# The first steps of a two-stream graph network in another written order

## The chip, the cores and the metric

The kernel runs on one core of one Trainium2 chip. The metric is the device time of one execution in microseconds; lower is better. Several runs of the same kernel are taken and their median is compared.

## The reference

There are 16 graphs (B) of 1024 nodes (N) with 128 features (C), and 4 layers (L) in each of two networks. All inputs are float32, and the adjacency holds zeros and ones.

```
h = relu(layernorm(x))
for i in range(4):                       # gated network
    m = adj^T @ (h @ weight[i])
    h = gru(m, h, w_ih[i], w_hh[i], b_ih[i], b_hh[i])
x = x + h * mask
h = relu(layernorm(x))
for i in range(4):                       # convolution with batch norm
    h = relu(adj @ (h @ W[i]) + b[i])
    h = gamma[i] * (h - mean) / sqrt(var + eps) + beta[i]   # over all graphs and nodes
x = x + h
```

In the GRU cell r and z are sigmoids, n is a tanh, and the new state is (1 - z) n + z h.

## The kernel before, in words

Features lie turned (channels on the 128 partitions, nodes along the free axis) for the gates, and by node for the aggregation. A 1024 x 1024 adjacency is held as 8 row tiles of 128 x 1024. The features are split into a high part in a reduced float format and a low part, both multiplied with the rows (`aggregate`, L511 to L522; 32 matmuls of 512 columns), so that the sum keeps float32 accuracy. That is exact only if the adjacency's values fit the reduced format; a "look" (L566 to L570, a maximum over the low 16 bits of a row on VectorE) records this for each of the 128 row tiles, and a general path that is not taken here stands behind it.

The gated network runs two streams, A (`sa`, even graphs) and B (`sb`, odd graphs), half a layer apart: while one stream aggregates, the other computes its gates. `gate_step` (from L700) makes six products for half of the nodes in four accumulators `g_r`, `g_hn`, `g_xn`, `g_z`; ScalarE takes the sigmoids (L730, L734) and the tanh (L733), VectorE the rest (L731, L732, L736 to L738). `half_step` repeats for the 16 graphs and 4 layers. The convolution follows, layer by layer over all graphs.

The change touches the opening alone, which is written out by hand for streams A and B with graphs 0 and 1. In it every engine works its queue in the order written (a manual schedule for all five engines); behind the opening only GpSimd and the DMA queue of SyncE are fixed, and a planner orders the other three. What the opening has to do:

- Load the x of both graphs, the small vectors (biases, scales, the mask: `load_small`, L431, issued on ScalarE's queue), the rows of graph 0, and the weights of layer 0. The first four rows of a graph land in a buffer `stage`, the other four in buffers of the tag `h`. The rows of graph 1 go to `stage` as well, one by one as those of graph 0 have been looked at and copied.
- Copy the rows to the reduced format (`open_rows`): those of graph 0 on GpSimd (0 to 3) and ScalarE (4 to 7), all of graph 1 on GpSimd.
- Norm both x (`norm_stats` on VectorE, then root, reciprocal, scale, and eight relus on ScalarE, four to a half), and split each half of y (`split_first`: a copy on ScalarE, L697, and a difference on VectorE, L698).
- Turn the small vectors on TensorE and copy them out on VectorE (`turn_small`: `vecs`, `brz`, `maskT`, L445 to L452), turn y of both graphs (`turn`, L603), and turn and combine the gate weights (`turn_layer`, L463 to L481: three copies to VectorE, one product, a fourth copy). All turns share two PSUM buffers.
- Fetch the x of graph 2 on GpSimd's queue, behind the row copies of graph 1 (`sa.ahead`; its issue is L531), for the norm that the planner puts beside the first gates.

At the very start TensorE turns the identity 52 times while it has nothing to do.

Of the kernel before, what the change touches and what calls it, by code (L numbers as in the profile page):

```python
# [16 lines left out]
P = 128  # L17
# [324 lines left out]
def exact_path(  # L342
# [21 lines left out]
    nc = tc.nc  # L364
    B, N, C = x.shape
    L = g_weight.shape[0]
    NB = N // P
    NH = N // HALF
    BH = HALF // P
# [12 lines left out]
    def tmp(name):  # L382
        return ps_t.tile([P, HALF], F32, tag="tmp", name=name)
# [5 lines left out]
    def flat(name):  # L389
        return keep.tile([P, NB, C], F32, tag="x", name=name, bufs=4)  # L390
# [10 lines left out]
    def hw_tiles(b, name):  # L401
        return [keep.tile([P, N], F32R, tag=f"hw{b % 2}{s}", name=f"{name}_{s}") for s in range(2)]


    ident = const.tile([P, P], F32, tag="ident", name="ident")
# [25 lines left out]
    def load_small(prep):  # L431

        vn = prep.tile([P, C], F32, tag="vn", name="vn", bufs=1)[:NV, :]
        r0 = 0
        for src in (g_b_ih, g_b_hh):
            nc.scalar.dma_start(vn[r0 : r0 + 3 * L, :], src.rearrange("l (g c) -> (l g) c", c=C))
            r0 += 3 * L
        for src in (c_b, c_gamma, c_beta):
            nc.scalar.dma_start(vn[r0 : r0 + L, :], src)
            r0 += L  # L440
        mn = prep.tile([P, P], F32, tag="mn", name="mn", bufs=1)
        nc.scalar.dma_start(mn, nodemask.rearrange("b (k p) -> (b k) p", p=P))
        return vn, mn

    def turn_small(vn, mn):  # L445
        pt = tmp("pt_v")
        nc.tensor.transpose(pt[:, :NV], vn, ident[:NV, :NV])
        nc.vector.tensor_copy(vecs, pt[:, :NV])
        nc.vector.tensor_add(brz, vecs[:, : 3 * L], vecs[:, 3 * L : 6 * L])
        pt = tmp("pt_m")  # L450
        nc.tensor.transpose(pt[:, :P], mn, ident)
        nc.vector.tensor_copy(maskT, pt[:, : B * NB])  # L452
# [72 lines left out]
    with ExitStack() as st:  # L525
# [3 lines left out]
        def load_x(b, eng):  # L529
            xt = flat(f"x{b}")  # L530
            eng.dma_start(xt, x[b].rearrange("(k p) c -> p k c", p=P))  # L531
            return xt
# [3 lines left out]
        def gru_row(b, j):  # L536
            if j < 6:
                return row_tile(f"row{b}_{j}")
            return work.tile([P, N], F32R, tag="row2", name=f"row{b}_{j}", bufs=4)

        def load_rows_first(b, stage):

            fs = []
            for j in range(NB):
                if j < 4:
                    f = stage[:, 2 * j : 2 * j + 2, :].rearrange("p a n -> p (a n)")
                else:
                    f = work.tile([P, N], F32, tag="h", name=f"first{b}_{j}", bufs=7)
                nc.sync.dma_start(f, adj[b][j * P : (j + 1) * P, :])
                fs.append(f)  # L550
            return fs
# [14 lines left out]
        def look(b, row, j):  # L566

            lows = row.bitcast(U16).rearrange("p (n t) -> p n t", t=2)[:, :, 0]
            k = b * NB + j
            nc.vector.tensor_reduce(low[:, k : k + 1], lows, axis=AX.X, op=ALU.max)  # L570
# [11 lines left out]
        def norm_stats(xt, name):  # L582
            stats = small.tile([P, NB, 6], F32, tag="ln_st", name=f"st_{name}")
            mv = small.tile([P, NB, 2], F32, tag="ln_mv", name=f"mv_{name}")
            for k in range(NB):
                nc.vector.bn_stats(stats[:, k, :], xt[:, k, :])
                nc.vector.bn_aggr(mv[:, k, :], stats[:, k, :])
            return mv

        def norm_apply(xt, y, name, mv, split=None):  # L590
            rs = small.tile([P, NB], F32, tag="ln_rs", name=f"rs_{name}")
            nc.scalar.activation(rs, mv[:, :, 1], AF.Sqrt, bias=eps_t)
            nc.vector.reciprocal(rs, rs)
            ms = small.tile([P, NB], F32, tag="ln_ms", name=f"ms_{name}")
            nc.vector.scalar_tensor_tensor(ms, mv[:, :, 0], -1.0, rs, ALU.mult, ALU.mult)
            for k in range(NB):
                nc.scalar.activation(
                    y[:, k * P : (k + 1) * P], xt[:, k, :], AF.Relu, bias=ms[:, k : k + 1], scale=rs[:, k : k + 1]
                )
                if split and k % BH == BH - 1:  # L600
                    split(k // BH)

        def turn(y, name, hT=None):  # L603

            if hT is None:
                hT = work.tile([P, N], F32, tag="h", name=f"h_{name}", bufs=7)
            for hf in range(NH):
                pt = tmp(f"pt_{name}_{hf}")
                for q in range(BH):
                    k = hf * BH + q  # L610
                    nc.tensor.transpose(pt[:, q * P : (q + 1) * P], y[:, k * P : (k + 1) * P], ident)
                nc.scalar.copy(hT[:, hf * HALF : (hf + 1) * HALF], pt)
            return hT
# [31 lines left out]
        class Stream:  # L645
# [5 lines left out]
            def open(self, xt):  # L651

                self.xt = xt
                self.y = work.tile([P, N], F32, tag=f"y{self.tag}", name=f"y_in{self.b}", bufs=1)
                self.mv = norm_stats(xt, f"in{self.b}")

            def open_split(self):

                self.hw = hw_tiles(self.b, f"ghw{self.b}_0")
                norm_apply(self.xt, self.y, f"in{self.b}", self.mv, self.split_first)  # L660

            def open_rows(self, fs, on_scalar):
                self.rows, self.looks = [], NB
                for j, f in enumerate(fs):
                    t = gru_row(self.b, j)
                    if j in on_scalar:
                        nc.scalar.copy(t, f)
                    else:
                        nc.gpsimd.tensor_copy(t, f)
                    self.rows.append(t)  # L670

            def prepare(self, b, xt):
# [126 lines left out]
        sa, sb = Stream(0), Stream(1)  # L799
        every = {getattr(mybir.EngineType, e) for e in ("PE", "DVE", "Activation", "Pool", "SP")}  # L800
        with tc.tile_pool(name="prep", bufs=1) as prep, tc.manual_schedule(engines=every):


            pt = tmp("pt_idle")
            for k in range(52):
                nc.tensor.transpose(pt[:, k % 4 * P : (k % 4 + 1) * P], ident, ident)
            x0, x1 = load_x(0, nc.sync), load_x(1, nc.sync)
            small_in = load_small(prep)
            stage = keep.tile([P, NB, N], BF16, tag="adjT", name="stage", bufs=1).bitcast(F32)
            rows0 = load_rows_first(0, stage)  # L810
            h0 = work.tile([P, N], F32, tag="h", name="h_in0", bufs=7)
            load_layer(0)
            w_g = flat("w_g")[:, :L, :]
            nc.sync.dma_start(w_g, g_weight.rearrange("l c d -> c l d"))

            sa.open(x0)
            sa.open_split()
            sb.open(x1)
            sa.open_rows(rows0, (4, 5, 6, 7))
            sa.agg_step(0)  # L820
            for j, f in enumerate(rows0):
                look(0, f, j)
            rows1 = load_rows_first(1, stage)
            for i in range(1, L):
                load_layer(i)
            h1 = work.tile([P, N], F32, tag="h", name="h_in1", bufs=7)
            sa.agg_step(1)
            turn_small(*small_in)
            turn(sa.y, "in0", h0)
            turn_layer(prep, w_g, 0)  # L830
            sa.hT = h0
            sb.open_split()
            turn(sb.y, "in1", h1)
            sb.hT = h1
            sb.open_rows(rows1, ())
            nc.gpsimd.dma_start(w_c, c_w.rearrange("l c d -> c l d"))
            sa.gate_step(0)
            sa.gate_step(1)
            sb.agg_step(0)
            sb.agg_step(1)  # L840
            for j, f in enumerate(rows1):
                look(1, f, j)
            for i in range(1, L):
                turn_layer(prep, w_g, i)
            sa.ahead()
        with tc.manual_schedule(engines={mybir.EngineType.Pool, mybir.EngineType.SP}):
            for s in range(1, B // 2 * L):
                half_step(sa, sb)
                half_step(sb, sa)
            sb.gate_step(0)  # L850
            sb.gate_step(1)
            with tc.issue_after(sb.last_act.ins):
                sa.rest()
            sb.finish()
# [4 lines left out]
    pt = tmp("pt_flag")  # L859
# [134 lines left out]
    for b in range(B):  # L994
        hT = conv_input(b, L, aff)
        for hf in range(NH):
            tag = turns[(b * NH + hf) % len(turns)]
            pt = tmp(f"pt_o{b}_{hf}") if tag == "tmp" else acc(tag, f"pt_o{b}_{hf}")
            for q in range(BH):
                k = hf * BH + q  # L1000
# [56 lines left out]
```

## Time and profile before

| | us |
|---|---|
| median of 3 runs | 1886.74 (1886.47 to 1887.95) |
| the profiled execution | 1884.96 |
| its span, first to last instruction | 1883.2 |
| TensorE busy with matmuls | 1826.3 (97%) |
| VectorE busy | 1209.0 (64%) |
| ScalarE busy | 1041.8 (55%) |
| GpSimd busy | 287.5 (15%) |
| mean granted TensorE clock | 0.986 |

The profile is of one execution. It names engines PE (TensorE matmul), PEld (its weight loads), DVE (VectorE), ACT (ScalarE), POOL (GpSimd) and SP (SyncE, which only issues DMAs); a q behind the name means the queue of DMA issues. Times count from the first instruction. A wait is named after what ended it. A busy TensorE is not TensorE at its peak, since the ends of matmuls are modelled. The opening with the gates of graph 0 takes the first 50 us of the span.

### The profile page before, as it was taken

The page shows a single profiled execution, that of the slowest core. Times are in us where ns is not written, and L with a number is a line of the kernel's source. Part 1 is how long each engine was busy: PE and PEld are TensorE (multiplying, and loading weights), DVE is VectorE, ACT ScalarE, POOL GpSimd, SP SyncE. Part 2 cuts the span into 40 slices and gives each one's busy share as a digit, 9 for nine tenths or more (in the row PEclk, how much of TensorE's full clock was granted, in tenths as well). Part 3 has the DMA queues.
Part 4 walks back from the last instruction along what each step waited for, and adds up shares of the span by engine and source line. Part 5 has one row for each costly group of instructions (what it writes and reads, how often), then busy time and mean ns, then how long its engine had stood idle before and what let it go on. Part 6 is the DMA issues. An engine that isn't in the chain of part 4 may idle for free.

```text
span 1883.2 us, 21902 instructions
## 1 busy us (share of the span) xinstructions
PE 1826.3 (97%) x7324; PEld 1259.9 (67%) x7324; DVE 1209.0 (64%) x2235; ACT 1041.8 (55%) x1561; POOL 287.5 (15%) x369
## 2 busy tenths in 40 slices
PE   7999999999999999999999999999989989989995
PEld 4666656666656566656665666667768878878884
DVE  5746864865784685595586476576656656665664
ACT  4354563563545454445456353476767767767764
POOL 3130230231141032033023012010100000000021
PEclk8999999999999999999999999999999999999997
DMA  7487476385386476557547536269956757675768
GB/s 258 120 229 255 157 203 216 140 223 170 134 256 189 147 190 202 200 168 234 190 157 203 208 114 169 85 220 319 305 187 214 246 179 246 223 247 180 250 208 259
DMA packets 267824, 381.21 MB, mean 202 GB/s; under 512 B 149716, under 2 KB 171896, under 8 KB 263864
## 3 DMA queue, kind: packets, MB, share of 16 engines
q1 hardware_dynamic: 250032, 246.21, 43.2%
q0 software_dynamic: 17456, 133.45, 20.2%
q8 instruction: 59, 0.97, 0.2%
q14 instruction: 61, 0.50, 0.1%
q10 hardware_dynamic: 216, 0.08, 0.0%
HBM read 287.39 MB, written 117.44 MB: 215 GB/s over the span
## 4 chain that ended last, share of the span: by engine, by line
PE 44%; issue 5%; DMA 3%; DVE 2%; POOL 1%; ACT 1%; SPq 0%; DVEq 0%; POOLq 0%; ACTq 0%
PE pc_m L516 12%; PE pc_g_r L516 5%; PE pc_g_z L516 5%; PE pm L516 5%; PE hw_c L493 5%; PE g_z L720 2%; PE g_r L720 2%; DMA adjT<-half 2%; PE g_xn L720 1%; PE g_hn L720 1%; PE pt_o L1001 1%; PE pw_g_hn L931 1%; PE pw_g_xn L931 1%; PE pc_g_r L503 1%; PE hw_g L491 0%
## 5 line engine op out<-in xcount | busy, mean ns | idle before, releaser
L516 PE MATMUL pm<-row,ghw 128*128 128x512 f32 x2048 | 505.0, 403 | 1.7 <-ACT ghw L697 1.7
L516 PEld LDWEIGHTS pm<-row,ghw 128*128 128x128 f32 x2048 | 383.4, 188 | 107.0 <-issue 31.6
L516 PE MATMUL pc_m<-wide,chw 128*128 128x512 f32 x1024 | 247.6, 396 | 0.0
L516 PEld LDWEIGHTS pc_m<-wide,chw 128*128 128x128 f32 x1024 | 190.7, 189 | 41.5 <-issue 3.8
L733 ACT ACTIVATE r<-r,vecs 128x512 f32<-128x512 f32 x128 | 92.3, 721 | 203.5 <-DVE r L732 203.4
L516 PE MATMUL pc_g_r<-wide,chw 128*128 128x512 f32 x464 | 185.8, 400 | 0.0
L516 PE MATMUL pc_g_z<-wide,chw 128*128 128x512 f32 x464 | 180.8, 390 | 0.0
L575 POOL CAST half<-row 128x1024 bf16<-128x1024 f32 x128 | 139.9, 1109 | 248.8 <-DMA adjT<-half 167.8
L878 DVE CAST wide<-packed 128x1024 fp32r<-128x1024 bf16 x160 | 110.5, 694 | 81.9 <-PE pc_m L516 62.4
L878 DVE CAST wide<-block 128x1024 fp32r<-128x1024 bf16 x160 | 110.4, 693 | 80.0 <-PE pc_g_z L516 42.2
L734 ACT ACTIVATE z<-g_z,brz 128x512 f32<-128x512 f32 x128 | 87.4, 683 | 121.5 <-PE g_z L720 121.5
L496 DVE TENSOR_TENSOR ghw<-hw_g,ghw 128x512 fp32r<-128x512 f32 x96 | 61.7, 683 | 122.7 <-ACT ghw L495 122.7
L720 PE MATMUL g_xn<-m,w_mT 128*128 128x512 f32 x256 | 131.7, 596 | 3.9 <-DVE r L732 3.9
L876 ACT CAST wide<-packed 128x1024 fp32r<-128x1024 bf16 x96 | 100.6, 1048 | 60.7 <-PE pc_g_z L516 30.1
L876 ACT CAST wide<-block 128x1024 fp32r<-128x1024 bf16 x96 | 100.6, 1048 | 60.2 <-PE pc_m L516 34.0
L720 PE MATMUL g_r<-m,w_mT 128*128 128x512 f32 x256 | 131.2, 594 | 0.0
L570 DVE TENSOR_REDUCE low<-row 128x1 f32<-128x1024 uint16 x112 | 130.9, 1201 | 0.0
L720 PE MATMUL g_z<-m,w_mT 128*128 128x512 f32 x256 | 130.7, 592 | 0.0
L730 ACT ACTIVATE r<-g_r,brz 128x512 f32<-128x512 f32 x128 | 87.8, 686 | 61.1 <-PE g_r L720 60.0
L736 DVE TENSOR_TENSOR h<-h,r 128x512 f32<-128x512 f32 x96 | 69.6, 725 | 78.7 <-ACT r L733 78.7
L731 DVE SCALAR_TENSOR_TENSOR r<-g_hn,vecs,r 128x512 f32<-128x512 f32 x128 | 95.1, 743 | 36.4 <-PE g_hn L720 19.1
L708 ACT COPY m<-pm 128x512 f32<-128x512 f32 x128 | 68.1, 583 | 89.4 <-PE pm L516 89.4
(128 smaller groups left out, 2767.8 us busy)
## 6 DMA issues: line engine op xcount, KB each, us to landing
packed<-adjT_d SPq DMA_DIRECT2D x256, 256.0 KB, 5.7
block<-adjT_d SPq DMA_DIRECT2D x256, 256.0 KB, 5.3
raw<-in_adj_dram POOLq DMA_DIRECT2D x112, 512.0 KB, 11.6
row<-raw SPq DMA_DIRECT2D x112, 512.0 KB, 6.1
adjT_d<-adjT POOLq DMA_DIRECT2D x16, 2048.0 KB, 7.2
xmid_d<-x POOLq DMA_DIRECT2D x16, 512.0 KB, 4.1
y<-ymid_d POOLq DMA_DIRECT2D x16, 512.0 KB, 6.1
xo<-xmid_d POOLq DMA_DIRECT2D x32, 256.0 KB, 6.4
```

The costliest lines, as they stand in the source:

```text
L493: nc.tensor.matmul(pt[:, q * P : (q + 1) * P], src, w, start=True, stop=True)
L516: nc.tensor.matmul(pm[hf], hw[s][:, j * P : (j + 1) * P], rows[j][:, hf * HALF : (hf + 1) * HALF], start=(j == 0 and s == 0), stop=(j == N ...
L570: nc.vector.tensor_reduce(low[:, k : k + 1], lows, axis=AX.X, op=ALU.max)
L575: nc.gpsimd.tensor_copy(t, row.bitcast(F32))
L720: nc.tensor.matmul(po, wT[:, i, g * C : (g + 1) * C], rhs, start=start, stop=stop)
L730: nc.scalar.activation(r, pr, AF.Sigmoid, bias=brz[:, 3 * i : 3 * i + 1])
L731: nc.vector.scalar_tensor_tensor(r, phn, b_hn(i), r, ALU.add, ALU.mult)
L733: nc.scalar.activation(r, r, AF.Tanh, bias=b_in(i))
L734: self.last_act = nc.scalar.activation(z, pz, AF.Sigmoid, bias=brz[:, 3 * i + 1 : 3 * i + 2])
L736: nc.vector.tensor_sub(ho, hin, r)
L876: nc.scalar.copy(r, t)
L878: nc.vector.tensor_copy(r, t)
```

## The change

- The turns of the small vectors move to the front: ahead of the first norm on TensorE and VectorE. Of the 52 idle turns 20 stand ahead of them and 28 behind.
- The looks at the rows of graph 0 no longer stand together behind the second graph's statistics: rows 0 and 1 are looked at between the first norm's scale and its first half, row 2 between the halves, rows 3 to 7 behind the second graph's scale.
- The second graph's scale and the first half of its norm stand ahead of the first aggregation's evacuation, its split and second half behind the turn of the first graph's y.
- The turn of the second graph's y moves behind the first gates.
- The looks at the rows of graph 1 leave the manual schedule: the planner places them, not before the last gate operation of graph 0.

`norm_apply` is cut into `norm_scale` and `norm_half` for this, and `open_split` becomes `open_half`; `open_rows` takes the row numbers and the engine of the copies, which stay as they were. No arithmetic changes.

```diff
-        def norm_apply(xt, y, name, mv, split=None):
+        def norm_scale(name, mv):
             rs = small.tile([P, NB], F32, tag="ln_rs", name=f"rs_{name}")
...
             nc.vector.scalar_tensor_tensor(ms, mv[:, :, 0], -1.0, rs, ALU.mult, ALU.mult)
-            for k in range(NB):
+            return rs, ms
+
+        def norm_half(xt, y, scale, hf):
+            rs, ms = scale
+            for k in range(hf * BH, (hf + 1) * BH):
                 nc.scalar.activation(
                     y[:, k * P : (k + 1) * P], xt[:, k, :], AF.Relu, bias=ms[:, k : k + 1], scale=rs[:, k : k + 1]
                 )
-                if split and k % BH == BH - 1:
-                    split(k // BH)
...
+            def open_half(self, g):
+
+                norm_half(self.xt, self.y, self.scale, g)
+                self.split_first(g)
...
-            for k in range(52):
-                nc.tensor.transpose(pt[:, k % 4 * P : (k % 4 + 1) * P], ident, ident)
+            def idle(n):
+                for k in range(n):
+                    nc.tensor.transpose(pt[:, k % 4 * P : (k % 4 + 1) * P], ident, ident)
...
+            idle(20)
+            turn_small(*small_in)
+            idle(28)
             sa.open(x0)
-            sa.open_split()
+            sa.scale = norm_scale("in0", sa.mv)
+            sa.open_rows(rows0, range(4), nc.gpsimd)
+            look(0, rows0[0], 0)
+            look(0, rows0[1], 1)
+            sa.open_half(0)
+            look(0, rows0[2], 2)
+            sa.open_half(1)
             sb.open(x1)
-            sa.open_rows(rows0, (4, 5, 6, 7))
-            sa.agg_step(0)
-            for j, f in enumerate(rows0):
-                look(0, f, j)
+            sa.open_rows(rows0, range(4, NB), nc.scalar)
+            sb.scale = norm_scale("in1", sb.mv)
+            for j in range(3, NB):
+                look(0, rows0[j], j)
             rows1 = load_rows_first(1, stage)
             for i in range(1, L):
                 load_layer(i)
             h1 = work.tile([P, N], F32, tag="h", name="h_in1", bufs=7)
+            norm_half(sb.xt, sb.y, sb.scale, 0)
+            sa.agg_step(0)
             sa.agg_step(1)
-            turn_small(*small_in)
             turn(sa.y, "in0", h0)
             turn_layer(prep, w_g, 0)
             sa.hT = h0
-            sb.open_split()
-            turn(sb.y, "in1", h1)
-            sb.hT = h1
-            sb.open_rows(rows1, ())
+            sb.split_first(0)
+            sb.open_half(1)
+            sb.open_rows(rows1, range(NB), nc.gpsimd)
             nc.gpsimd.dma_start(w_c, c_w.rearrange("l c d -> c l d"))
             sa.gate_step(0)
             sa.gate_step(1)
+            turn(sb.y, "in1", h1)
+            sb.hT = h1
             sb.agg_step(0)
             sb.agg_step(1)
-            for j, f in enumerate(rows1):
-                look(1, f, j)
             for i in range(1, L):
                 turn_layer(prep, w_g, i)
             sa.ahead()
+        with tc.issue_after(sa.seen.ins):
+            for j, f in enumerate(rows1):
+                look(1, f, j)
```

More of the change, by code (lines that the diff above doesn't have):

```diff
@@ L599, in norm_apply @@
                 )
-                if split and k % BH == BH - 1:
-                    split(k // BH)
+        def norm_apply(xt, y, name, mv):
+            scale = norm_scale(name, mv)
+            for hf in range(NH):
+                norm_half(xt, y, scale, hf)
         def turn(y, name, hT=None):
@@ L655, in open, with open_rows @@
                 self.mv = norm_stats(xt, f"in{self.b}")
-            def open_split(self):
                 self.hw = hw_tiles(self.b, f"ghw{self.b}_0")
-                norm_apply(self.xt, self.y, f"in{self.b}", self.mv, self.split_first)
-            def open_rows(self, fs, on_scalar):
                 self.rows, self.looks = [], NB
-                for j, f in enumerate(fs):
+            def open_half(self, g):
+                norm_half(self.xt, self.y, self.scale, g)
+                self.split_first(g)
+            def open_rows(self, fs, js, eng):
+                for j in js:
                     t = gru_row(self.b, j)
-                    if j in on_scalar:
-                        nc.scalar.copy(t, f)
+                    if eng is nc.scalar:
+                        nc.scalar.copy(t, fs[j])
                     else:
-                        nc.gpsimd.tensor_copy(t, f)
+                        eng.tensor_copy(t, fs[j])
                     self.rows.append(t)
```

## The prediction

> **What bounds the kernel now.** I read the page's 40 slices first, then PE's waits (waiting engine, tile and line, releaser: us in total, times, longest), then the timeline and the busy stretches of the first 82 us, then the DMA issues there.
>
> ```profile
> PE   7999999999999999999999999999989989989995
> PEclk8999999999999999999999999999999999999997
> ```
>
> ```profile
> PE hw_c L493 <- ACT bn L897: 15.1, 3, 5.1
> PE pt_in L611 <- DVE vecs L448: 6.9, 1, 6.9
> ...
> PE pt_in L611 <- ACT y_in L597: 2.8, 2, 2.2
> PE pm L516 <- ACT ghw L697: 1.7, 1, 1.7
> ```
>
> TensorE is full in all slices but the first and the last; only the first (47 us) has real holes inside the part that the diff touches, and it alone runs at a reduced clock. The waits name them: 6.9 us for `vecs`, 2.8 us for the second graph's norm. So at most about 12 us lie here. What is won at TensorE by 75 us should stay won: its 2048 aggregation matmuls waited 1.7 us in all, and the other waits are 3.9 us for DVE and the phase borders.
>
> ```profile
> 2.79 0.38 ACTq L442 DMA_DIRECT2D mn<-in_nodemask_dram  x1
> ...
> 5.00 0.29 DVE L586 BATCH_NORM_STATS2 st_in<-x 128x6 f32<-128x128 f32 x1 [4.09 <-DMA x<-in_x_dram]
> ...
> 17.74 4.56 DVE L570 TENSOR_REDUCE low<-stage 128x1 f32<-128x1024 uint16 x4
> ...
> 22.22 4.59 DVE L570 TENSOR_REDUCE low<-first 128x1 f32<-128x1024 uint16 x4
> ...
> 26.73 0.18 DVE L448 COPY vecs<-pt_v 128x36 f32<-128x36 f32 x1
> ...
> 33.05 0.56 DVE L481 COPY w_mT<-pt_wm 128x384 f32<-128x384 f32 x1 [1.74 <-PE pt_wm L480]
> ...
> 35.48 0.90 POOL L531 DMA_DIRECT2D x<-in_x_dram  x1
> ...
> 38.88 1.91 PE L720 MATMUL g_r<-h_in,w_hhT 128*128 128x512 f32 x2
> ...
> 40.70 0.29 DVE L586 BATCH_NORM_STATS2 st_in<-x 128x6 f32<-128x128 f32 x1 [2.97 <-DMA x<-in_x_dram]
> ```
>
> ```profile
> mn<-in_nodemask_dram ACTq DMA_DIRECT2D x1, 64.0 KB, 5.0
> ```
>
> Columns of the timeline: start, duration, engine, line; the last line is from the DMA issues, with size and time to landing. Eight looks (1.14 us apart) keep DVE from `vecs` until 26.73; the weights are turned by 33.6, yet the first gates start at 38.88, behind the second norm and its turn. Two lines matter later: the mask lands 5.0 us after 2.79, and DVE stands still for 2.97 us until `x` of graph 2 lands at 40.7.
>
> [...] TensorE empties at 20.05, the granted clock falls to 0.50 within 24 to 25, and is back within 41 to 42. [...] `vecs`, whose input was there at 19.8, sat behind the looks for 7 us. [...]
>
> **The change, part by part.**
>
> *Small vectors first (turn_small ahead of the norm).* PE is given 48 idle turns for 52 (4 x 0.17 us, hidden in its wait for the split: without that wait 0.7 us). It removes the 6.9 us hole. But `maskT` now stands ahead of the x0 statistics on DVE. The mask lands at 2.79 + 5.0 = 7.8; turn 0.33 and copy 0.28 with hand-overs: 8.6 instead of 5.0. **The first norm starts 3.6 us later.** Statistics 3.27 (5.00 to 8.27), root to scale 1.1 (8.30 to 9.38), four relus 1.65 and cast 0.62: the first aggregation starts at 15.4, not 11.86.
>
> *Looks spread.* DVE from 13.0: two looks (2.3) end at 15.3, just as the first cast does, so the split is not late; look 2, second split (its cast ends 17.5): 18.3; x1 statistics 3.26: 21.5. ACT: four row casts after 17.5 take 4.2: 21.7; the last row's matmuls end 1.3 later (as 18.35 to 19.6 now), 23.0. The root of x1 (22.0), scale (22.9), looks 3 to 7 (5 x 1.14): 28.6. Then `w_hhT` 0.56, `w_ihT` 0.56, `w_gT` 0.28, the product 0.8 warm to 1.65 cold, `w_mT` 0.56: **first gates at 31.7, against 38.88: 7.2 us earlier.** ACT's second norm half, split and table load (1.28) all end by about 32; they cost nothing, since the DVE chain covers them. So does it cover the copy of the turned x0, whose buffer is that of an earlier row and which may wait for look 5 (26.4): without that cover it would be up to 1.5 us (ACT free at 25). TensorE has holes from 25 to 31 and may be cold here.
>
> *What does not move along: x of graph 2.* Its load is issued on POOL behind the eight row casts of graph 1. SP loads those rows in order, and row 3 waits for look 3, which now ends at 24.0 (about 22.3 before); rows 4 to 7 are behind it on SP. A row after a quiet queue takes 4.0 us (19.01 to 23.02), the next ones 1.28 each (the casts from 29.70): 24.1 + 4.0 + 4 x 1.28 = 33.2, up to 34.3 with the weight loads between (33.6 before). POOL then casts and issues w_c: x at +1.86, 35.1, and lands 5.2 later: **40.3 (38.6 to 41.2); before 40.7.** In the new order its statistics stand on DVE behind the first L731 and ahead of the first L732. So L732 (0.69) waits for 40.6 and ends 41.3; behind it on ACT tanh (0.72) and then z (0.69): 42.7. PE's second `g_z` needs that bank: two products of 0.86: gates end 44.5. Unhindered they would end at 31.7 + 12 x 0.86 = 42.0, or 44 from a cold start, so the clock costs nothing more while this wait covers it. Before: 50.06. **5.6 us earlier.**
>
> *Second turn behind the gates.* Eight turns, 1.0: aggregation 45.5 to 53.3 (50.06 to 57.85): **4.5 earlier.** Its rows (cast by 34.3) and split (by 34) wait ready.
>
> *Looks of graph 1, free on DVE after the last gate.* DVE is never idle from 40.3: eight statistics 3.0, ten gate operations 7.0: looks from 50.3 (52.72 before), only **2.4 earlier**. The order has six looks (6.9), then `w_hhT`: 57.7. PE has turned both weights and done `g_r` by 55.2 and needs a free turn buffer for `pt_g`: it waits 2.5. Then on DVE `w_ihT`, look, `w_gT`, look, L731, `w_mT`: 0.56 + 1.14 + 0.28 + 1.14 + 0.75 + 0.56 = 4.4, 62.1, which the next layer's turn awaits, while PE has about 4 us of work. Walking both queues on, graph 0's second aggregation starts at 71.9. The same walk over the old order comes out 0.3 too late against the trace's 74.04, so I take 71.8: 2.2 earlier. One `g_r` pair (0.86) that was done ahead of it before is now behind it: **1.4 us won.** SP's and POOL's queues are in the old order throughout, the other three from here on. The looks of graph 1 also free the buffer for the first turned adjacency; POOL's casts for it came at 77.8, so looks that end near 60 cost nothing there; they would from about 74.
>
> Sum: 7.2 at the gates, 5.6 at their end, 4.5 behind the aggregation, 1.4 when DVE has caught up. The profiled execution took 1884.96 (span 1883.2 and 1.8 around it); it would take 1883.6. The three runs have a median 1.8 above it, so 1886.74 - 1.4 = **1885.3**. About 0.2%, 3.8 us, is what a measurement of this kernel can tell from no change.
>
> **Rivals.**
> - *x of graph 2 lands early enough.* Every microsecond before 40.3 is won whole, since it heads the DVE chain, until about 36, where PE is the limit again. For: rows 0 to 2 are loaded well before, so only five rows remain. Against: row 3 leaves later than before, and no load of x took under 4.2 us. From 38.0 the gain passes 3.8; at 36.5 it is 5.2: 1881.5.
> - *The small vectors land late: slower.* Place: `maskT`, at the head of DVE's queue. The mask's landing at 7.8 is one sample; every microsecond later delays norm, look 3, row 3 and x of graph 2 alike. Break-even at 9.2; beyond 0.2% from 13.0. For: it competes with x and rows, and such rows took up to 9.2 us. Against: nothing ahead of it changes in the queues. At 13.2: 1890.7.
> - *Nothing arrives at the end*: a phase border swallows the shift, 1886.7. Against: the borders wait for PE's own last results.
>
> **How the numbers follow.** Forecast 0.58 (own range 1882.6 to 1887.2: x from 38.6 to 41.2 gives -1.7 to +0.9, and about 1 us for the walk), early x 0.2, nothing arriving 0.12, late mask 0.1. Range 1881.5 to 1889: the early case whole, the late one up to 11.5. Faster by over 0.2%: 0.2; within: 0.7; slower: 0.1.
>
> **What would show it.** Right: first statistics at about 8.6; aggregation near 15.4; no 6.9 us wait for `vecs`; gates near 31.7; DVE waiting for `x` for about 6 us between the first L731 and L732; `g_xn` or `g_z` waiting there; looks of graph 1 from about 50; `pt_g` waiting for `w_hhT`. Wrong: x of graph 2 before 38, or DVE idle ahead of the looks of graph 1 (PE, not DVE, would then set the pace), or the norm still starting near 5.

## The result and the profile after

The changed kernel takes 1885.04 us (median of 12 runs, 1883.13 to 1885.80), the kernel before in the same comparison 1887.96 us (12 runs, 1885.69 to 1888.87). The ratio is 0.9987, 95% interval [0.9978, 0.9996]: 2.5 us faster, between 0.8 and 4.2. The forecast was 1885.3 us, 1.4 us faster than before.

The profiled execution of the changed kernel took 1885.67 us (span 1883.9), that of the kernel before 1884.96 (1883.2). This one pair alone would say "0.7 us slower", so it is no measure of the gain; it serves to place things inside the opening. The turn of graph 2's x starts at 132.30 us before and 130.40 after, 1.9 us earlier; the last such turn (graph 15, at 1055.5) is 0.6 us earlier, and the stretch from there to the end lasts 827.1 us before and 828.4 after. Over all the profiles of this study that last stretch lasted 826.8 to 829.9 us with no visible relation to the edits, all of which lie in the first 70 us. So medians over many runs carry the verdicts, and the profiles the places.

The row of TensorE's granted clock (in tenths of full speed) in the page's 40 slices, changed kernel:

```profile
PEclk9999999999999999999999999999999999999998
```

The first slice, 8 before, is a 9 now. That need not be the change's doing: in two executions of one kernel below (the one with both later edits) the granted clock from 25 to 31 us was 0.50 in one and 1.00 in the other. TensorE's waits in the whole run (waiting tile, its line, what ended the wait: us in total, times, longest), the last line from the kernel before:

```profile
PE g_xn L728 <- DVE r L740: 7.4, 11, 1.9
...
PE pt_whh L467 <- ACT h_in L619: 2.9, 1, 2.9
...
PE pt_g L476 <- DVE w_hhT L468: 1.8, 2, 1.1
```

```profile
PE g_xn L720 <- DVE r L732: 3.9, 8, 0.6
```

The 6.9 us for `vecs` and the 2.8 us for the second graph's norm are not in the list any more. In their place stand 2.9 us for the copy of the turned x0 (it waits for a look, since its buffer is that of an earlier row), one wait of 1.9 us of `g_xn` for L740 (the old L732; before, the longest of 8 such waits was 0.6 us, 3.9 in all), and 1.1 us of `pt_g` for `w_hhT`. The mask, from the DMA issues (size in KB, us to landing):

```profile
mn<-in_nodemask_dram ACTq DMA_DIRECT2D x1, 64.0 KB, 5.6
```

VectorE's timeline (start, duration, engine, line, operation; in brackets the idle time before it and what ended it):

```profile
9.25 0.28 DVE L586 BATCH_NORM_STATS2 st_in<-x 128x6 f32<-128x128 f32 x1
...
24.23 4.58 DVE L570 TENSOR_REDUCE low<-first 128x1 f32<-128x1024 uint16 x4
...
36.07 0.75 DVE L739 SCALAR_TENSOR_TENSOR r<-g_hn,vecs,r 128x512 f32<-128x512 f32 x1 [1.71 <-PE g_hn L728]
41.71 0.29 DVE L586 BATCH_NORM_STATS2 st_in<-x 128x6 f32<-128x128 f32 x1 [4.89 <-DMA x<-in_x_dram]
42.23 0.69 DVE L740 TENSOR_TENSOR r<-g_xn,r 128x512 f32<-128x512 f32 x1 [0.23 <-DVE st_in L586]
...
50.52 4.59 DVE L570 TENSOR_REDUCE low<-stage 128x1 f32<-128x1024 uint16 x4
```

TensorE's:

```profile
31.63 1.92 PE L728 MATMUL g_r<-h_in,w_hhT 128*128 128x512 f32 x2
...
70.96 2.40 PE L516 MATMUL pm<-row,ghw 128*128 128x512 f32 x8
```

And the looks at graph 1's rows and graph 0's second aggregation before:

```profile
52.72 4.59 DVE L570 TENSOR_REDUCE low<-stage 128x1 f32<-128x1024 uint16 x4
...
74.04 7.56 PE L516 MATMUL pm<-row,ghw 128*128 128x512 f32 x32
```

Read them as a relay. The first statistics start at 9.25 (5.00 before), the first gates at 31.63 (38.88 before): 7.2 us ahead. VectorE then stands still for 4.89 us until x of graph 2 has landed, and the first L740, which stands behind the first of the statistics and whose inputs were there at 36.8, starts at 42.23; the looks at graph 1's rows start at 50.52 (52.72 before): 2.2 ahead. Graph 0's second aggregation starts at 70.96 (74.04 before), 3.1 ahead, of which 0.86 is a pair of `g_r` that now stands behind it instead of ahead of it: 2.2 us won. Of the 7.2 us at the gates 5.0 are handed back by the time the looks start, across the wait for x of graph 2.

### The profile page after: what moved, and what is told of

It reads as the page before. It is cut to its first block, busy times and chain, and to the rows that moved or that the text cites. A ratio compares the mean times of both kernels' runs of the same rounds, so it can differ in the third digit from the quotient of the medians.

```text
span 1883.9 us, 21894 instructions
## 1 busy us (share of the span) xinstructions
PE 1826.3 (97%) x7320; PEld 1261.2 (67%) x7320; DVE 1214.1 (64%) x2235; ACT 1040.3 (55%) x1561; POOL 288.0 (15%) x369
## 3 DMA queue, kind: packets, MB, share of 16 engines
q1 hardware_dynamic: 250032, 246.21, 43.3%
q0 software_dynamic: 17456, 133.45, 20.1%
## 5 line engine op out<-in xcount | busy, mean ns | idle before, releaser
L742 ACT ACTIVATE z<-g_z,brz 128x512 f32<-128x512 f32 x128 | 87.3, 682 | 115.8 <-PE g_z L728 115.8
L739 DVE SCALAR_TENSOR_TENSOR r<-g_hn,vecs,r 128x512 f32<-128x512 f32 x128 | 95.0, 742 | 38.5 <-PE g_hn L728 21.2
L493 PE MATMUL hw_c<-w_c,bn 128*128 128x128 f32 x768 | 100.5, 287 | 15.1 <-ACT bn L920 15.1
```

Source lines behind the costliest of these rows:

```text
L493: nc.tensor.matmul(pt[:, q * P : (q + 1) * P], src, w, start=True, stop=True)
L739: nc.vector.scalar_tensor_tensor(r, phn, b_hn(i), r, ALU.add, ALU.mult)
L742: self.last_act = nc.scalar.activation(z, pz, AF.Sigmoid, bias=brz[:, 3 * i + 1 : 3 * i + 2])
```

## The experiments

All ratios are to the kernel before, measured on the same chip. "Second aggregation" is the start of graph 0's second aggregation in the one profile of each kernel.

| kernel | second aggregation, us | ratio, 95% interval | runs |
|---|---|---|---|
| before | 74.04 | 1 | |
| the change | 70.96 | 0.9987 [0.9978, 0.9996] | 12 |
| change, x of graph 2 early | 63.45 | 0.9958 [0.9945, 0.9972] | 5 |
| change, small vectors behind the first scale | 68.28 | 0.9974 [0.9966, 0.9982] | 13 |
| both of these, first and second time | 63.07, 60.44 | 0.9933 [0.9919, 0.9947], 0.9935 [0.9922, 0.9949] | 5, 5 |
| before, x of graph 2 early | 74.88 | 0.9999 [0.9990, 1.0007] | 13 |
| change, second turn ahead of the gates again | 69.21 | 0.9978 [0.9971, 0.9985] | 18 |
| change, looks of graph 0 together again | 74.51 | 1.0014 [1.0007, 1.0021] | 21 |
| change, half of graph 1's looks left out | 70.81 | 0.9976 [0.9970, 0.9983] | 21 |
| both, with idle turns, first and second time | 60.82, 61.55 | 0.9939 [0.9925, 0.9953], 0.9934 [0.9920, 0.9947] | 5, 5 |
| before, small vectors at the front alone | 77.63 | 1.0016 [1.0010, 1.0023] | 21 |
| change, second norm back | 68.73 (2 of 32 products; the others from 69.73) | 0.9973 [0.9962, 0.9983] | 8 |

In the kernels with the early x, and in those that undo a part of the changed kernel or leave looks out, an explicit order keeps the statistics of graph 2's x where they stand anyway: behind the first L739, or, in the kernel before, behind the second graph's first split. The code cuts below leave it out. It moves the lines behind it: L740 is L742 in those made from the changed kernel, save the ones with idle turns.

### Is x of graph 2 what the new order waits for?

The load is issued on GpSimd ahead of the row copies of graph 1 instead of behind them:

```diff
+            sa.next_x = load_x(2, nc.gpsimd)
             sb.open_rows(rows1, range(NB), nc.gpsimd)
...
-                if self.i == 1:
+                if self.i == 1 and self.b > 0:
                     self.next_x = load_x(self.b + 2, nc.gpsimd)
```

> The changed kernel with one load moved: x of graph 2 is issued on POOL ahead of the row copies of graph 1, not behind them; VectorE's order stays that of the changed kernel. Theory (the wait for this x between the first L731 and the first L732 sets the pace from 37 us on): x lands before 25, VectorE goes from the first gate operation to the next without the 4.9 us wait, the first gates end near 43 instead of 46, looks of graph 1 start near 46 instead of 50.5, graph 0's second aggregation starts near 67 instead of 71.0: 4 us less, ratio to the kernel before about 0.9966. Rival (VectorE's sum of work, or TensorE's half clock in these gates, sets the pace and x only happens to be late): the second aggregation stays within 1 us of 71.0, ratio 0.9987 as for the change.

The same edit in the kernel before:

> The kernel before with only the load of x of graph 2 issued ahead of the row copies of graph 1; its statistics stay behind the second graph's first split on VectorE. Theory (in the old order that wait of 3 us lies under the gates, whose start and products TensorE sets): the wait for x is gone, gates start at 38.9 and end at 50 as before, looks of graph 1 start at 52 to 52.7, second aggregation of graph 0 at 73.5 to 74, ratio 0.9997 to 1.0000. Rival (the wait for x limits both orders): 2 to 3 us less, ratio about 0.9987.

Measured: 1878.08 us and 0.9958 in the new order, 0.9999 in the old one. VectorE's line in the new order with the early x:

```profile
42.52 2.34 DVE L570 TENSOR_REDUCE low<-stage 128x1 f32<-128x1024 uint16 x2
```

And TensorE's second aggregation of graph 0:

```profile
63.45 2.86 PE L516 MATMUL pm<-row,ghw 128*128 128x512 f32 x10
```

The looks start at 42.52 for 50.52, and no statistics wait for x. The second aggregation comes 7.5 us sooner in this pair of profiles; the medians say 5.5. The same transfer, moved by the same edit, is worth nothing before and 5.5 us after (0.9987 - 0.9958 = 0.0029 of 1887). In the old order the second norm and its turn held the gates until 38.88, and x, there at 40.7, came in their shadow; the change moved these away and left x as the last to arrive.

### What do the small vectors at the front cost?

In the changed kernel they go behind the first scale, so that the first norm need not wait for the mask:

```diff
-            idle(20)
-            turn_small(*small_in)
-            idle(28)
+            idle(48)
             sa.open(x0)
             sa.scale = norm_scale("in0", sa.mv)
+            turn_small(*small_in)
```

> The changed kernel with the small vectors' turn one step later: behind the first norm's scale, ahead of the first look; 48 idle turns stand together. Theory (the mask, which landed at 8.4, holds back the first statistics and through look 3 and row 3 also x of graph 2): first statistics at 5.0 instead of 9.25, first aggregation near 12.4 instead of 15.8, look 3 ends near 20.7 instead of 24.2, x lands near 38.2 instead of 41.7, second aggregation of graph 0 near 67.5: 3.5 us less, ratio about 0.9968. Rival (rows of graph 1 are held by the DMA engines and not by the look): x stays at 41 to 42 and the second aggregation at 70 to 71, ratio 0.9987, although the norm starts at 5.0.

Measured 0.9974, where the theory had 0.9968; the interval touches that of the changed kernel, so the size of the gain is loose. The statistics start at 5.01 again, and x lands at 38.45 for 41.71:

```profile
38.45 0.29 DVE L586 BATCH_NORM_STATS2 st_in<-x 128x6 f32<-128x128 f32 x1 [7.95 <-DMA x<-in_x_dram]
```

Look 3, at whose end row 3 of graph 1 can be loaded, ends at 20.3 for 24.3, 4 us sooner, and x 3.3 us; VectorE's wait for it grows from 4.89 to 7.95 us. The opposite test takes only this part of the change into the kernel before: `turn_small` at the front between 20 and 28 idle turns, and gone from behind `agg_step(1)`.

> The kernel before with one part of the change alone: the turns of the small vectors (and maskT) at the front, 20 idle turns ahead and 28 behind them. Theory: the 6.9 us wait for vecs is gone, yet the first norm starts 3.5 to 4 us later (statistics at 8.6 to 9.3 for 5.0) and with it the looks, which still stand together, so that rows 3 to 7 of graph 1 and x of graph 2 come 3 to 4 us later (x at 43.5 to 45 for 40.7); graph 0's second aggregation at 76 to 78 for 74.0, ratio 1.0008 to 1.0022. Rival, the wait for vecs was on the path and its 6.9 us are won in part whatever the rest does: second aggregation at 70 to 73, ratio 0.9978 to 0.9995.

Measured 1.0016: 3.0 us slower than before. The 6.9 us wait for `vecs` was gone, yet the gates started at 38.92 (38.88 before). The copy of `w_hhT`, the gates, and the x of graph 2 in this kernel:

```profile
30.62 0.55 DVE L468 COPY w_hhT<-pt_whh 128x384 f32<-128x384 f32 x1
```

```profile
38.92 1.91 PE L720 MATMUL g_r<-h_in,w_hhT 128*128 128x512 f32 x2
```

```profile
44.61 0.49 DVE L586 BATCH_NORM_STATS2 st_in<-x 128x6 f32<-128x128 f32 x2 [6.81 <-DMA x<-in_x_dram]
```

Two things cancel at the gates. The late norm pushes the eight looks, which still stand together, 3.9 us back, so that `w_hhT` is copied behind them at 30.62; before, the looks were done at 26.8, but the wait for `vecs` held this copy until 29.74. From there on the product, the second norm and its turn follow in both kernels. And x of graph 2 comes 3.9 us later. So the removal of the old profile's largest wait does not pay in this form. What it is worth without the late norm, this run does not show. The place of the small vectors at the front costs the changed kernel some 2.5 us (0.0013).

### Both together

> Both edits of the two runs above in the changed kernel. Theory: the two delays lie in one chain behind each other, so with x out of the way the earlier norm still counts: gates of graph 0 start near 28 instead of 31.6, end near 39.5, graph 0's second aggregation starts near 63.5, 7.5 us less than the change, ratio about 0.9948. Rival (they are two causes of the same wait, so removing either removes it): no more than the better of the two alone, second aggregation near 67, ratio 0.9966.

Measured 0.9933, and 0.9935 when it was run again, a larger gain than the 0.9948 of the theory, and far from the rival's 0.9966: 12.5 us faster than the kernel before, the best version of this study and 10 us faster than the changed kernel. What each edit brings alone (0.0029 and 0.0013) makes 0.0042 of the 0.0054 for both, and each interval reaches 0.0008 to 0.0014 to either side: they add up, within what can be told.

### Which of the other parts earns something?

Spread of the looks undone (looks 0 to 2 go back behind the second scale, to the other five):

```diff
-            look(0, rows0[0], 0)
-            look(0, rows0[1], 1)
             sa.open_half(0)
-            look(0, rows0[2], 2)
             sa.open_half(1)
...
-            for j in range(3, NB):
+            for j in range(NB):
                 look(0, rows0[j], j)
```

> The changed kernel with the spread of looks 0 to 2 undone: all 8 looks at graph 0's rows stand together behind the second scale, the norm and the turn stay where the change put them. Theory: the two splits come 1.7 to 3.4 us sooner (the aggregation starts at 14 or so for 15.8, as far as the norm's scale lets it), but the row slots of graph 0 come free in the same order later, so that graph 1's last cast, and with it the load of x, moves by -0.5 to +1.5 us; graph 0's second aggregation follows it, 70.5 to 72.5, ratio 0.9984 to 0.9996. Rival, the spread is what the change's gain comes from: looks 3 to 7 and w_hhT's copy end later by the 3.4 us that were spread, the gates with them, second aggregation at 73 or later, ratio 0.9997 to 1.0005.

Measured 1.0014. The rival was right and my expectation wrong:

```profile
15.63 0.69 DVE L706 TENSOR_TENSOR ghw<-y_in,ghw 128x512 fp32r<-128x512 f32 x1 [2.36 <-ACT ghw L705]
17.84 0.69 DVE L706 TENSOR_TENSOR ghw<-y_in,ghw 128x512 fp32r<-128x512 f32 x1 [1.52 <-ACT ghw L705]
```

The splits did not come sooner (aggregation at 15.74 for 15.76; ScalarE's cast sets it), so looks 0 to 2 (3.4 us) had lain in VectorE's waits for ScalarE, which are now bare (2.36 and 1.52 us ahead of the two L706), and were free. Behind the second scale they push the end of looks 3 to 7 to 31.4, all rows of graph 1 behind the first look, and x of graph 2 to 45.20:

```profile
45.20 0.29 DVE L586 BATCH_NORM_STATS2 st_in<-x 128x6 f32<-128x128 f32 x1 [5.49 <-DMA x<-in_x_dram]
```

In the changed kernel the spread is worth 5.1 us (0.0027): without it the other parts make the kernel slower than before. What it brings alone, in the kernel before, was not run.

Second norm undone: the scale and both halves of the second norm go behind `turn_layer` again.

```diff
-            sb.scale = norm_scale("in1", sb.mv)
             for j in range(3, NB):
                 look(0, rows0[j], j)
...
-            norm_half(sb.xt, sb.y, sb.scale, 0)
             sa.agg_step(0)
...
-            sb.split_first(0)
+            sb.scale = norm_scale("in1", sb.mv)
+            sb.open_half(0)
             sb.open_half(1)
```

> The changed kernel with one part undone: the scale and the first half of the second graph's norm stand behind the turned weights of layer 0 again; small vectors, spread of looks and late turn stay. Theory, x of graph 2 sets the pace: looks 3 to 7 need not stand behind the wait for the second scale, start at 21.6 for 23.1, and row 3 of graph 1 leaves 1.5 us sooner, so that x lands at 40 to 40.8 for 41.7; the later norm (split ended by 36 to 37) stays inside the wait for x, second aggregation at 69 to 70, ratio 0.9976 to 0.9984. Rival: the norm's eight relus and two splits keep ScalarE and VectorE from the first gate operations: gates stall, second aggregation at 71.5 to 74, ratio 0.9990 to 1.0000.

Measured 0.9973. Look 3 and x in this kernel:

```profile
21.56 1.19 DVE L570 TENSOR_REDUCE low<-stage 128x1 f32<-128x1024 uint16 x1
...
40.54 0.29 DVE L586 BATCH_NORM_STATS2 st_in<-x 128x6 f32<-128x128 f32 x1 [2.04 <-DMA x<-in_x_dram]
```

Look 3 starts at 21.56 for 23.10 because it no longer stands behind the second scale, and x lands 1.2 us sooner. (On the 0.84 us that this scale took there, see the last section.) The later norm delays the first L739 to 37.75 (36.07), which the wait for x still covers: it shrinks from 4.89 to 2.04 us.

Second turn undone: it stands ahead of the gates again.

```diff
+            turn(sb.y, "in1", h1)
+            sb.hT = h1
             sa.gate_step(0)
             sa.gate_step(1)
-            turn(sb.y, "in1", h1)
-            sb.hT = h1
             sb.agg_step(0)
```

> The changed kernel with one of its three edits undone: the turn of the second graph's y stands ahead of the first gates again (8 turns and two copies of h_in on ScalarE). My theory, that the load of x for graph 2 sets the pace behind the first gates: the gates start 1 to 3 us later (32.6 to 34.5 for 31.6), which ends inside the 4.9 us for which VectorE waits for x; L740's first instruction stays at 42 to 42.5, the aggregation of graph 1 at 46.5 to 47.5, graph 0's second aggregation at 70.5 to 71.5, ratio to the kernel before 0.9984 to 0.9991. Rival, TensorE's own work sets the stretch: 1 to 3 us are lost, second aggregation at 72 to 74, ratio 0.9992 to 1.0000.

Measured 0.9978: I had expected the same time as the changed kernel's, and it is about 1.7 us less. The gates start later (33.07) and finish behind the same wait for x, which covers the turn. Two lines of VectorE show where the gain is:

```profile
40.93 0.29 DVE L586 BATCH_NORM_STATS2 st_in<-x 128x6 f32<-128x128 f32 x1 [3.89 <-DMA x<-in_x_dram]
...
55.39 0.55 DVE L468 COPY w_hhT<-pt_whh 128x384 f32<-128x384 f32 x1
```

x is there 0.8 us sooner, and the copy of `w_hhT` comes 1.9 us sooner (57.28 in the changed kernel): the planner, which counts with its own times, put five looks of graph 1 ahead of it instead of six. The same five stand ahead of it in the kernel with the second norm back. So about 1 us of what each of these two gains comes from the planner's list. Why x was 0.8 us sooner was not settled. The copy of graph 1's last row, ahead of it on GpSimd, started at 33.23 for 34.84; in the kernel with half the looks below, the same up to there but for one store to `low`, it started at 34.99, so this may differ from one execution to the next. The intervals of both kernels overlap that of the changed kernel at their ends ([0.9978, 0.9996]), so that these two parts cost something is likely rather than certain; no gain from them is to be seen.

The parts don't simply add up. By these runs the spread is worth 5.1 us, and the small vectors, the second norm and the second turn cost 2.5, 2.6 and 1.7: together a loss of 1.7, where the change gains 2.5. So each figure holds only with the other parts in place. The last part, graph 1's looks left to the planner, was not undone.

### Is VectorE's list the limit behind x?

Looks 4 to 7 of graph 1 are left out, and their four columns are set to zero at the start:

```diff
+            nc.gpsimd.memset(low[:, NB + 4 : 2 * NB], 0.0)
             idle(20)
...
-                look(1, f, j)
+                if j < 4:
+                    look(1, f, j)
```

> The changed kernel with looks 4 to 7 at graph 1's rows left out (their four columns are set to zero on GpSimd at the start, so the check of those four rows for low halves is not made); the planner also orders the copies and gate operations behind them anew. Theory, that once x has landed VectorE's list (statistics, gate operations, looks of 1.15 us each, copies of the next layer's turned weights) sets the time: w_hhT's copy comes 2 to 3.5 us sooner than 57.3, graph 0's second aggregation at 67.5 to 69.5 for 71.0, ratio 0.9970 to 0.9980. Rival, TensorE's gates and aggregation set it whatever VectorE does: 70.5 to 71.2, ratio 0.9984 to 0.9990.

Measured 0.9976, as the theory said, but the profile has the second aggregation at 70.81, as the rival said. Its TensorE shows why the two don't agree:

```profile
43.27 2.08 PE L728 MATMUL g_xn<-m,w_mT 128*128 128x512 f32 x2 [3.18 <-DVE r L742]
45.14 1.79 PE L728 MATMUL g_z<-h_in,w_hhT 128*128 128x512 f32 x2
```

In this execution the granted clock went to 0.50 at 43.3, behind the wait for x, and these two pairs took 2.08 and 1.79 us for 1.13 and 1.12 in the changed kernel's profile: 1.6 us. That is enough to hide a gain of this size. From the start of graph 1's aggregation to graph 0's second one it is 22.4 us here (48.42 to 70.81) and 24.0 in the changed kernel (46.92 to 70.96), but that does not show what the looks are worth either: the kernel with graph 0's looks together, whose gates were also slow at that place (pairs of 1.78 and 1.91 us), takes 22.4 with all eight looks of graph 1 (52.11 to 74.51). A later start shortens the stretch by itself, since VectorE's list is then further on. What is left is the time of 21 runs, which says 2 us, with intervals that touch, and the wait of 1.1 us for `w_hhT` in the changed kernel. So VectorE's list is likely a limit there, by up to 1.6 us. At 22.4 us TensorE has no wait left in the stretch: none stands in its timeline from 41.06 to 63.45 in the kernel with the early x, and the kernels made from the changed one with that edit take 22.4 to 22.7.

### Is a cold TensorE the next cost?

In the kernel with both edits the first gates ran at half clock (0.50 from 25.0 to 31.85, 1.91 us a pair). That idle turns in the holes ahead of them would prevent it was a guess, which no run had shown: 14 behind the turn of y, and 8, 4 and 4 inside `turn_layer`.

```diff
             turn(sa.y, "in0", h0)
-            turn_layer(prep, w_g, 0)
+            warm = acc("g_z", "warm")
...
+            def keep_warm(n):
+                for k in range(n):
+                    nc.tensor.transpose(warm[:, k % 4 * P : (k % 4 + 1) * P], ident, ident)
...
+            keep_warm(14)
+            turn_layer(prep, w_g, 0, keep_warm)
```

> The kernel with both later edits (x of graph 2 loaded early, the small turns behind the first scale) and 30 idle turns on TensorE in the holes between the first aggregation and the first gates: 14 behind the turn of the first y, 8 behind pt_wih, 4 behind pt_g, 4 behind pt_wm. Theory: the gates at half clock cost that kernel 1.5 to 2.5 us, since its granted clock was 0.50 from 25 to 31 us and its two first g_r took 1.91 us each for 0.86 to 1.02 warm; with the turns the clock stays up, g_r takes 0.86 to 1.0, the aggregation of graph 1 starts at 38.5 to 39.5 for 40.7, ratio 0.9918 to 0.9928 for 0.9933. Rivals: VectorE's list sets it, no change (0.9931 to 0.9936); or idle turns do not hold the clock, or come in the weights' way, and it is slower by 0.5 to 2 us (0.9936 to 0.9944).

The second aggregation started at 60.82 for 63.07, and the time did not fall: 0.9939. Both kernels were run once more:

> The kernel with both later edits (x of graph 2 loaded early, small turns behind the first scale) once more, beside the kernel with the idle turns, since two single profiles showed a cold clock in one and not in the other: ratio 0.9926 to 0.9940, first gates at half clock again if the cold stretch belongs to the order and not to the single execution; second aggregation at 62.5 to 63.5, without the cold stretch at 61.

> The same with the 30 idle turns, once more. If the 2.2 us that its profile showed at graph 0's second aggregation arrive at the end, the ratio is 0.0008 to 0.0014 below that of the kernel without them; if they are lost behind the opening, the two are equal within 0.0005. Second aggregation at 60.5 to 61.2.

0.9935 without and 0.9934 with the turns. TensorE's first gates in the two executions of the kernel without them:

```profile
27.37 1.91 PE L728 MATMUL g_r<-h_in,w_hhT 128*128 128x512 f32 x2
29.08 1.91 PE L728 MATMUL g_r<-m,w_mT 128*128 128x512 f32 x2
```

```profile
26.61 1.02 PE L728 MATMUL g_r<-h_in,w_hhT 128*128 128x512 f32 x2
27.46 1.08 PE L728 MATMUL g_r<-m,w_mT 128*128 128x512 f32 x2
```

One kernel, two profiles: 1.91 us a pair, then 1.02 and 1.08. In the second one TensorE was cold in the first aggregation for longer instead: its clock from 15 to 19 us was 0.63, 1.00 in the first, and the aggregation took 10.46 us for 9.05. So the order alone does not make the gates cold, and comparing single profiles had made a gain of them. With the idle turns these gates took 1.02 us a pair in the second execution (1.02 and 1.08 without them), and the turns bring nothing that can be measured.

## Why the prediction was right, step by step

- **First norm.** Statistics forecast at 8.6, measured 9.25; the mask took 5.6 us to land where the profile before had 5.0, which is the difference (the turn of the mask that waits for it starts at 8.56 here, at 8.38 in the kernel with the early x and at 7.88 in the one with the second norm back). Aggregation 15.4 forecast, 15.76 measured. That this part costs time is borne out both ways: 3.0 us lost when it is done alone, about 2.5 us won when it is undone.
- **Looks and first gates.** Look 3 ends at 24.3 (24.0), looks 3 to 7 at 28.7 (28.6), gates 31.63 (31.7). The wait of the copied x0 for a look, which the prediction named as covered by the VectorE chain, is there (2.9 us) and covered. The clock was 0.50 from 28.0 to 34.8, and that cost nothing, as forecast: `g_xn` waited for L740 all the same.
- **x of graph 2.** Forecast 40.3 (38.6 to 41.2), measured 41.71, outside by 0.5. Its issue was at 36.70 instead of 35.1: the last row of graph 1 landed later than the "up to 34.3" (its copy started at 34.84). VectorE waited 4.89 us (about 6), and L740 stayed behind the statistics all that time: that VectorE keeps to the order written, on which the count rests, held there. This term was mis-sized by 1.4 us, and the gates with it: they end at 46.1 (44.5), and graph 1's aggregation starts at 46.92 (45.5).
- **VectorE behind x.** Forecast 10.0 us until the looks, measured 8.8 (41.71 to 50.52): the eight statistics and ten gate operations were added up at full length, while in the trace the next one starts before the recorded end of the last (L746 at 45.40 lasts 0.68, L739 starts at 46.00). 1.2 us too much; it hides the miss on x, so that the looks start at 50.52 where 50.3 was forecast.
- **Behind the looks.** `w_hhT` at 57.28 (57.7), `pt_g` waits 1.1 us (2.5), second aggregation 70.96 (71.8). The net gain there is 2.2 us, not 1.4: the third mis-sized term, the wait of `pt_g`.
- **The rivals.** The early x did not happen by itself; made to happen, it brought 7.9 us against the kernel before (0.0042), more than the 5.2 that the prediction gave for an x at 36.5, about where it had TensorE as the next limit; the mechanism was the one stated. The late mask came at 8.4, short of the break-even of 9.2. That a phase border swallows the shift is not borne out: 0.8 us at least arrive.
- **The number.** That 1885.3 lies 0.3 us from the median is in part luck. Its base, three runs with the median 1886.74, lay 1.2 us below the twelve of the comparison; against these the gain was 2.5 us for 1.4. And inside the opening a miss of 1.4 us on x was cancelled by one of 1.2 us behind it.

So the mechanism held: the gain at the gates, the wait that takes its place, and the short rest. What the prediction did not see is that two of the parts (the second norm ahead of the looks, which it priced at nothing, and the turn behind the gates, at 1.0 us) bring nothing that can be seen and likely make the kernel slower, and that without the three looks in VectorE's idle time the change would be a loss.

## What to carry to other kernels

When a reordering frees an engine early, ask which transfer lies in the shadow of what you moved away: here the load that was worth nothing in the old order (0.9999) was worth 5.5 us in the new one, for a small edit. Undo the parts of a bundle one at a time: without one part this change was a loss, with another undone it was some 2.5 us faster, and two more brought nothing. And trust no single profile for 2 us where the clock can differ between executions, as here (1.91 and 1.02 us for the same pair): run the kernel again, or count medians.

## What the runs showed of the hardware

Five stretches at half clock in the opening lasted 3.4 to 17.1 us. From the clock of narrow windows (0.50 inside, 1.00 around): 16.7 to 20.1 in the kernel with the second turn ahead and 43.3 to 46.7 in the one with half the looks (3.4 us each), 28.0 to 34.8 in the changed kernel and 25.0 to 31.85 in the one with both edits (6.8), 24.4 to 41.45 in the kernel before (17.1). They lay in different places in two executions of the same kernel, the one with both edits: from 25 to 31 us the clock was 0.50 in the first and 1.00 in the second, from 15 to 19 us 1.00 and 0.63. What sets their length and place was not tested.

The start needs care. The 28 idle turns behind the mask took 5.91 us in the changed kernel's profile and 3.22 in that of the kernel with the early x, which is the same up to there, while the windows read a clock of 1.00 from 5 to 14 us in the changed kernel. Its trace holds no record of the clock before 14.3 us, and 1.00 is shown where there is none. There the duration of an instruction of known size tells more: a pair of gate products took 1.91 us at a clock of 0.50 and 1.02 at 1.00.

A small operation of VectorE lasted until a copy on GpSimd ended. The scale of a norm (L595 in most of the kernels), 128 by 8 values, took 0.17 us at 18.82 in the second execution of the kernel with both edits, where GpSimd was idle from 15 to 19 us. In the changed kernel's second norm it took 0.84:

```profile
22.34 0.84 DVE L595 SCALAR_TENSOR_TENSOR ms_in<-mv_in,rs_in 128x8 f32<-128x8 f32 x1
```

```profile
22.12 1.04 POOL L677 CAST row<-stage 128x1024 fp32r<-128x1024 f32 x1 [0.23 <-DMA stage<-in_adj_dram]
```

It ends at 23.18, just behind the row copy on GpSimd (23.16). So it is with both scales of the kernel before (8.87, 0.51 us, and 33.75, 0.93 us), which end 0.02 us behind a row copy (9.36 and 34.66), and with the second one of the kernel with the small vectors at the front alone (34.47, 0.24 us; the copy ends at 34.70). What makes them wait was not tested. It shows in the first norm: with the small vectors at the front alone the statistics start at 8.44 instead of 9.25 and the first aggregation at 15.75 instead of 15.76, since the scale took 0.96 us there (12.31 to 13.27) and 0.17 in the changed kernel (13.12 to 13.29).
